# Layer 3 attention: one-bank units beside the scores, spread by a TensorE budget, with heads in another order

## The chip, the cores and the metric

One Trainium2 chip, of which the kernel uses one core. The metric is the device time of one execution in microseconds. The kernel before takes 4210.45 us, the median of three runs (4210.17 to 4224.06).

## The reference, cut to what matters

The program is a four-layer network on an input of 8 samples, 256 channels and 32 x 32 pixels, so 1024 tokens of 256 values in each sample. Everything is in fp32. The change lies in the attention of the last layer and in the routing of its mixture of experts:

```python
def _L3_attn_ref(x, qkv_w, qkv_b, proj_w, proj_b):   # x: (8, 1024, 256), normalised tokens
    ...                                              # 8 heads of 32
    scores = jnp.einsum('bnhd,bmhd->bhnm', q, k) * scale
    t = jnp.square(scores + C_SHIFT)                 # C_SHIFT = 5
    attn = t / jnp.sum(t, axis=-1, keepdims=True)
    out = jnp.einsum('bhnm,bmhd->bnhd', attn, v).reshape(B, N, D)
    return out @ proj_w.T + proj_b
...
t = t + _L3_attn_ref(_ln_t(t), ...)
t = t + _L3_ffn_ref(_ln_t(t), ...)                   # top 2 of 8 experts for each token
```

A weight of the attention is the square of a shifted score, so there is no exponential and no row maximum. The sum over keys of such squares is a quadratic form of q, and the kernel gets it from the 32 x 32 matrix of k times k, without summing the squares themselves.

## The kernel before, in words

`fast3` (from L2518) is the attention stage of layer 3. In the profiled execution it runs from about 2870 to 3842 us of the span. After it `fast3e` runs the experts to the end.

**A sample's attention.** `attention(b)` has 32 steps for a sample: two halves of the queries (`hh`, 512 each), two chunks of four heads (`c`), eight tiles of 128 keys (`kt`). Step i issues four score matmuls `s<-q,k` (L2684), one for each head on its own 32 rows of the array, into two PSUM pairs. A pair is two banks, 128 x 1024 fp32, for two heads. Two ACT squares `e<-s,five` of 128 x 1024 (L2690) empty them. Then `values(i - 1)` issues the four matmuls `A<-e,v` (L2668) of the step before, each on 32 columns of the array. I call the four matmuls of a step a quad. Eight steps add up in one bank A. After these, DVE writes `o<-A,r` (L2673), a product with the reciprocal r of the sum. After each second such group `proj` (L78 with `wo`) of four tiles goes into a pair, and DVE adds it to x (L2679).

**Work beside it.** While sample b runs, the generator `between(b)` prepares others, in this order:

- `routes.route(b - 1)` (from L2378) normalises the tokens of the sample just finished (`token_norm_steps`: statistics on DVE, `tn_r` on ACT, `mo_x` on DVE), adds them to x on POOL, sends both to DRAM, transposes them (`mo_xT`), computes the router's logits (`mo_l`), and then has a chain: a softmax (DVE, one exp on ACT, DVE), five DVE operations for the rank of each expert, choice and weights (to `both`), the counts `mo_n` on PE, and `cnt`, then sixteen small DVE operations that fill `place` and `carry`.
- `norm(b + 1)` loads x, normalises it to `xt` and transposes it to `xn`.
- `projections(b + 1)` makes q and k (`qk`, evacuated by ACT), v (by DVE), transposes of k (`kT`), G (products of k with itself), `Gq` (G times q, evacuated into `prod` by DVE) and `D` (the sum over a head, evacuated by ACT's Ln and turned round by Exp). Its two `D` evacuations also send r to DRAM.

In sample 0 `routes.fill()` follows, which issues eight large transfers `so<-zero` on SP.

**Order and PSUM.** Instructions stay on each engine in an order fixed when the program is built, except that the scheduler may move unpinned ones. `spread` (L1067) runs `attention(b)` and `between(b)` side by side, one count of yields against another: `between` has 19 yields for projections and 12 for route, over the 33 of a sample. After each sample everything left over is issued before the next begins. PSUM has three pairs (`own["S"]`, 6 banks), shared by the scores and everything beside them, and two one-bank buffers for A.

```python
def pair(name):
    return net.lent["pair"](name) if not own else own["S"].tile([P, 2, HF], F32, tag="S", name=name)

def bank(name):
    return pair(name)[:, 0]
```

`bank` is used before for G alone and takes a whole pair, using half.

Of the kernel before, what the change touches and what calls it, by code (L numbers as in the profile page):

```python
# [2306 lines left out]
class Routes:  # L2307
# [70 lines left out]
    def route(self, b, x, ones, pair):  # L2378
# [14 lines left out]
        for c in range(KC):  # L2393
            ps = pair("mo_xT").rearrange("p h n -> p (h n)")
            for t in range(NT):
                nc.tensor.transpose(ps[:, bass.ts(t, P)], xn[:, t, bass.ts(c, P)], net.ident)
            nc.vector.tensor_copy(xk[:, c, :], ps)
            yield

        pr = two.tile([P, NT, E8], F32, tag="pr", name="pr")  # L2400
        for t4 in range(0, NT, 4):
            ps = pair("mo_l")[:, 0]
            for i in range(4):
                net.linear(ps[:, bass.ts(i, E8)], xk, self.wr, bass.ts(t4 + i, P), slice(0, E8))
            nc.vector.tensor_copy(pr[:, t4 : t4 + 4], ps[:, : 4 * E8].rearrange("p (t e) -> p t e", e=E8))
            if not t4:
                yield
# [36 lines left out]
        ps = pair("mo_n")[:, 0]  # L2444
# [73 lines left out]
def fast3(net, io):  # L2518
# [4 lines left out]
    with ExitStack() as ctx, ExitStack() as tok, ExitStack() as att, ExitStack() as bef:  # L2523
# [41 lines left out]
        def norm(b):  # L2565
            x = xs[b] = xpool.tile([P, NT, C], F32, tag="x", name="x")

            (nc.sync if b else nc.scalar).dma_start(out=halves(x), in_=tokens(io.src[b]))
            yield
            xt = one.tile([P, NT, C], F32, tag="xt", name="xt")  # L2570
            yield from net.token_norm_steps(xt, x, norms, b > 0)
            yield
            xn = xns[b] = one.tile([P, KC, N], F32, tag="xn", name="xn")
            for c in range(KC):
                ps = pair("xn")
                for t in range(NT):
                    nc.tensor.transpose(ps[:, t // 4, bass.ts(t % 4, P)], xt[:, t, bass.ts(c, P)], net.ident)
                nc.vector.tensor_copy(xn[:, c, :], ps.rearrange("p h n -> p (h n)"))
                yield
            nc.gpsimd.tensor_tensor(x, x, bo.unsqueeze(1).to_broadcast([P, NT, C]), ALU.add)  # L2580

        def projections(b):
            xn = xns.pop(b)
            for d, w, bias, name in ((qs, wq, bq, "q"), (ks, wkk, bk, "k")):
                d[b] = own["two"].tile([P, KC, N], F32, tag=name, name=name)
                for c in range(KC):
                    ps = pair("qk")
                    for h in range(2):
                        net.linear(ps[:, h], w, xn, bass.ts(c, P), bass.ts(h, HF))
                    nc.scalar.activation(d[b][:, c, :], ps.rearrange("p h n -> p (h n)"), AF.Identity, bias=bias(c))  # L2590
                    yield
            v = vs[b] = own["two"].tile([P, NT, C], F32, tag="v", name="v")
            for t4 in range(0, NT, 4):
                ps = pair("v")
                for i in range(4):
                    net.linear(ps[:, i // 2, bass.ts(i % 2, C)], xn, wv, bass.ts(t4 + i, P), slice(0, C))
                nc.vector.tensor_copy(
                    v[:, t4 : t4 + 4].rearrange("p t c -> p (t c)"), ps.rearrange("p h n -> p (h n)")
                )
                yield  # L2600

# [3 lines left out]
            for t4 in range(0, NT, 4):  # L2605
                ps = pair("kT")
                for i in range(4):
                    for c in range(KC):
                        nc.tensor.transpose(
                            ps[:, i // 2, (i % 2) * C + c * P : (i % 2) * C + (c + 1) * P],  # L2610
                            ks[b][:, c, bass.ts(t4 + i, P)], net.ident,
                        )
                nc.vector.tensor_copy(
                    kt[:, t4 : t4 + 4, :, :P], ps.rearrange("p h (i c n) -> p (h i) c n", c=KC, n=P)
                )
                yield
            G = bank("G").rearrange("p (c n) -> p c n", c=KC)
            for c in range(KC):
                for t in range(NT):
                    nc.tensor.matmul(  # L2620
                        G[:, c, : P + 1], lhsT=kt[:, t, c, :P], rhs=kt[:, t, c, : P + 1],
                        start=(t == 0), stop=(t == NT - 1),
                    )
            gm = own["k2"].tile([P, KC, P + 4], F32, tag="gm", name="gm")
            nc.vector.tensor_tensor(gm[:, :, : P + 1], G[:, :, : P + 1], heads.to_broadcast([P, KC, P + 1]), ALU.mult)
            yield
            prod = one.tile([P, KC, N], F32, tag="xt", name="prod")
            r = rs[b] = own["two"].tile([P, KC, N], F32, tag="r", name="r")
            for c in range(KC):
                ps = pair("Gq")  # L2630
                for h in range(2):
                    nc.tensor.matmul(
                        ps[:, h], lhsT=gm[:, c, :P], rhs=qs[b][:, c, bass.ts(h, HF)], start=True, stop=True
                    )
                nc.vector.scalar_tensor_tensor(
                    prod[:, c, :], ps.rearrange("p h n -> p (h n)"), gm[:, c, P : P + 1], qs[b][:, c, :],
                    ALU.add, ALU.mult,
                )
                yield
            for c in range(KC):  # L2640
                ps = pair("D")
                for h in range(2):
                    nc.tensor.matmul(
                        ps[:, h], lhsT=heads[:, 0, :P], rhs=prod[:, c, bass.ts(h, HF)], start=True, stop=True
                    )
                nc.scalar.activation(
                    r[:, c, :], ps.rearrange("p h n -> p (h n)"), AF.Ln, scale=SCALE * SCALE, bias=rest
                )
                nc.scalar.activation(r[:, c, :], r[:, c, :], AF.Exp, scale=-1.0)
                nc.sync.dma_start(out=net.sums3[8 * b + 4 * c : 8 * b + 4 * c + 4, :], in_=r[0:P:32, c, :])  # L2650
                yield

        def attention(b):
            q, k, v, x = qs[b], ks[b], vs[b], xs[b]
            o = own["o"].tile([P, KC, N], F32, tag="o", name="o")
            steps = [(hh, c, kt) for hh in range(2) for c in range(KC) for kt in range(NT)]
            es, accs = {}, {}

            def values(i):
                hh, c, kt = steps[i]  # L2660
# [3 lines left out]
                if first:  # L2664
                    accs[0] = own["A"].tile([P, HF], F32, tag="A", name="A")
                A = accs[0]
                for h in range(NH):
                    nc.tensor.matmul(  # L2668
                        A[32 * h : 32 * h + 32], lhsT=v[:, kt, c * P + 32 * h : c * P + 32 * h + 32],
                        rhs=e[:, h, :], start=first, stop=last,  # L2670
                    )
                if last:
                    nc.vector.tensor_tensor(o[:, c, cols], A, rs[b][:, c, cols], ALU.mult)  # L2673
                    if c == KC - 1:
                        ps = pair("proj")
                        for t in range(4):
                            net.linear(ps[:, t // 2, bass.ts(t % 2, C)], o, wo, bass.ts(4 * hh + t, P), slice(0, C))
                        xh = x[:, 4 * hh : 4 * hh + 4].rearrange("p t c -> p (t c)")
                        nc.vector.tensor_tensor(xh, ps.rearrange("p h n -> p (h n)"), xh, ALU.add)  # L2679

            for i, (hh, c, kt) in enumerate(steps):
                ss = [pair("s") for _ in range(2)]
                for h in range(NH):
                    nc.tensor.matmul(  # L2684
                        ss[h // 2][:, h % 2], lhsT=k[32 * h : 32 * h + 32, c, bass.ts(kt, P)],
                        rhs=q[32 * h : 32 * h + 32, c, bass.ts(hh, HF)], start=True, stop=True,
# [6 lines left out]
                yield  # L2693
            values(len(steps) - 1)
            yield


        ROUTE = 12

        def between(b):  # L2700

            if b:
                yield from routes.route(b - 1, xs[b - 1], one, pair)
# [5 lines left out]
            else:  # L2709
                yield from net.head()  # L2710
# [8 lines left out]
        own["S"], own["A"] = io.pool(att, "f3s", 3, PSUM), io.pool(att, "f3v", 2, PSUM)  # L2719
        own["k1"], own["k2"] = io.pool(bef, "f3k", 1), io.pool(bef, "f3g", 2)  # L2720
        for _ in projections(0):
            pass
        for b in range(B):
            if b == B - 1:
                bef.close()
            beside = [(between(b), 19 * (b + 1 < B) + (ROUTE if b else 6))]
            for g, (first, last) in enumerate(GROUPS[:-1]):
                if b == last + 1:
                    beside.append((routes.sort(g), 1 + NT * (last - first)))
            spread((attention(b), 33), beside)  # L2730
        att.close()
        routing = routes.route(B - 1, xs[B - 1], one, lambda name: net.lent["pair"](name))
# [503 lines left out]
```

## Time and profile before

| what | value |
|---|---|
| time, median of 3 runs | 4210.45 us (4210.17 to 4224.06) |
| profiled execution, its own time | 4221.38 us |
| its span, mean granted clock of TensorE | 4219.6 us, 0.952 |
| PE, DVE, ACT, POOL busy over the span | 92%, 54%, 54%, 13% |
| layer 3 attention (first s to last step) | about 2870 to 3842 us |
| experts | 3842 to 4219.6 us |

Times inside the span are counted from its start. A matmul of fp32 leaves two records in the trace, so a quad of four heads is "x8". The profiler models the ends of matmuls and a few records are missing, so a busy PE is not always a PE at work; the start of one group to the start of the next is the safer measure. "idle before" names what the instruction waited for. A line such as `L78 PE MATMUL qk<-xn,w_l_wq` is the helper `linear`, and the names of the tiles tell which unit it is.

### The profile page before, as it was taken

How to read it: one execution, taken by the hardware profiler on the slowest of the kernel's cores; microseconds unless marked ns; L12 is line 12 of the kernel's file. 1: busy time of each engine (PE TensorE's matmuls, PEld its weight loads, DVE VectorE, ACT ScalarE, POOL GpSimd, SP SyncE). 2: the span in 40 equal slices, each digit the busy share in tenths (PEclk: the TensorE clock that was granted, in tenths of full speed). 3: DMA queues.
4: the chain of work that ended last, by engine and by line, in shares of the span. 5: the costliest groups of instructions: out<-in, count | busy, mean ns of one | idle time of the engine just before them, and what ended most of it. 6: DMA issues, size and time to landing. Idle time of an engine off the chain costs nothing. (4 is left out here: it accounts for less than half of the span.)

```text
span 4219.6 us, 52288 instructions
## 1 busy us (share of the span) xinstructions
PE 3866.5 (92%) x19430; PEld 1900.2 (45%) x19430; DVE 2297.3 (54%) x3994; ACT 2259.1 (54%) x3030; POOL 563.7 (13%) x645
## 2 busy tenths in 40 slices
PE   7999999999987788879999978989899999999997
PEld 3223333333333344444444435654344443436986
DVE  2368878878897488963222255842223333314455
ACT  3455655655554367743433445624655566666554
POOL 0000000000000000000000012440000050124763
PEclk9999999999998788889999989999999999999998
DMA  2222232232212468740100012430700040126676
GB/s 88 62 73 70 73 107 80 73 107 70 70 70 101 147 217 290 254 155 0 41 20 21 22 58 83 148 129 15 226 31 10 27 144 34 36 93 196 197 246 217
DMA packets 212346, 432.70 MB, mean 103 GB/s; under 512 B 26633, under 2 KB 137180, under 8 KB 199668
## 3 DMA queue, kind: packets, MB, share of 16 engines
q1 hardware_dynamic: 188980, 377.70, 27.1%
q0 software_dynamic: 19440, 46.45, 3.3%
q10 hardware_dynamic: 3664, 5.11, 0.4%
q8 instruction: 157, 2.57, 0.3%
q14 instruction: 105, 0.86, 0.1%
HBM read 257.56 MB, written 153.89 MB: 98 GB/s over the span
## 5 line engine op out<-in xcount | busy, mean ns | idle before, releaser
L2690 ACT ACTIVATE e<-s,five 128x1024 f32<-128x1024 f32 x512 | 538.8, 1110 | 277.9 <-PE s L2684 277.0
L1246 DVE SCALAR_TENSOR_TENSOR a<-hp,w_f_vec,a 128x961 f32<-128x961 f32 (+1 forms) x496 | 608.2, 1232 | 104.9 <-ACT a L1239 96.3
L2684 PE MATMUL s<-q,k 32*128 32x512 f32 x2048 | 348.6, 641 | 14.5 <-ACT e L2690 12.0
L1353 DVE TENSOR_TENSOR sum<-sum,e 128x1024 f32<-128x1024 f32 x192 | 230.4, 1218 | 149.2 <-ACT e L1399 149.2
L1399 ACT ACTIVATE e<-s 128x1024 f32<-128x1024 f32 x256 | 249.7, 1022 | 91.5 <-PE s L1393 82.1
L2668 PE MATMUL A<-e,v 128*32 128x512 f32 x2048 | 277.6, 606 | 0.3 <-ACT e L2690 0.3
L1357 PE MATMUL A<-e,va 128*32 128x512 f32 x2048 | 275.8, 620 | 0.0
L78 PE MATMUL pi<-xn,w_l_wpi 128*128 128x512 f32 x512 | 240.1, 610 | 13.7 <-ACT u L1500 9.2
L2684 PEld LDWEIGHTS s<-q,k 32*128 32x128 f32 x2048 | 111.4, 183 | 177.4 <-issue 94.2
L1393 PE MATMUL s<-q,k 32*128 32x512 f32 x1024 | 182.2, 648 | 2.4 <-ACT e L1399 2.4
L2837 PE MATMUL h<-xk,w 128*128 128x128 f32 x1192 | 152.7, 283 | 13.8 <-DVE xk L2823 13.8
L1704 PE MATMUL acc<-wt,z 128*64 128x192 f32 (+4 forms) x1344 | 128.5, 335 | 39.8 <-DVE wt L1759 39.3
L1026 POOL DMA_INDIRECT res<-y,to x149 | 148.6, 997 | 110.5 <-DVE y L2861 58.2
L78 PEld LDWEIGHTS pi<-xn,w_l_wpi 128*128 128x128 f32 x512 | 93.6, 193 | 149.5 <-issue 112.1
L2837 PEld LDWEIGHTS h<-xk,w 128*128 128x128 f32 x1192 | 150.6, 199 | 18.9 <-DVE xk L2823 14.1
L2806 ACT COPY w<-w_l3f_w 128x512 f32 x149 | 92.6, 625 | 115.8 <-PE h L2837 111.3
L1307 POOL MEMSET thrice<- 32x128 f32 x32 | 6.3, 196 | 1072.6 <-PE pe L1324 1072.6
L1438 ACT ACTIVATE hp<-pi,pib 128x512 f32<-128x512 f32 x128 | 87.1, 690 | 115.9 <-PE pi L78 115.9
L1324 PE MATMUL pe<-thrice,w_f_wpe 96*32 96x496 f32 (+1 forms) x768 | 130.7, 615 | 17.0 <-DMA thrice<-v 10.2
L2857 PE MATMUL y<-w_l3f_w,hid 128*128 x596 | 142.2, 381 | 0.3 <-ACT hid L2843 0.3
L1026 POOL DMA_INDIRECT so<-xl,rows x128 | 129.8, 1014 | 91.2 <-issue 50.4
L1357 PEld LDWEIGHTS A<-e,va 128*32 128x32 f32 x2048 | 61.9, 112 | 175.9 <-issue 175.3
(406 smaller groups left out, 6978.6 us busy)
## 6 DMA issues: line engine op xcount, KB each, us to landing
row<-shifts SPq DMA_DIRECT2D x144, 512.0 KB
x<-d SPq DMA_DIRECT2D x31, 1024.0 KB
xs<-so SPq DMA_DIRECT2D x73, 260.0 KB
so<-zero SPq DMA_DIRECT2D x5, 3380.0 KB
thrice<-v SPq DMA_DIRECT2D x256, 64.0 KB
gated<-st SPq DMA_DIRECT2D x32, 512.0 KB
hc<-gated SPq DMA_DIRECT2D x32, 512.0 KB
xl<-mox SPq DMA_DIRECT2D x64, 256.0 KB
```

What stands on the lines that cost most here:

```text
L78: self.nc.tensor.matmul(ps, lhsT=w[:, i, m], rhs=src[:, i, cols], start=(i == 0), stop=(i == k - 1))
L1026: made = self.nc.gpsimd.indirect_dma_start(**args)
L1246: nc.vector.scalar_tensor_tensor(to, fr, taps(t_), to, ALU.mult, ALU.add)
L1353: nc.vector.tensor_tensor(half, half, e[j], ALU.add)
L1357: nc.tensor.matmul(state["A"][32 * h : 32 * h + 32, c, :], lhsT=vas[b][:, kt, c, 32 * h : 32 * h + 32], rhs=e[h // 2][:, h % 2, :], start= ...
L1393: nc.tensor.matmul(ss[h // 2][:, h % 2], lhsT=ks[b][32 * h : 32 * h + 32, bass.ts(kt, P)], rhs=qs[b][32 * h : 32 * h + 32, bass.ts(gq, HF) ...
L1399: nc.scalar.activation(es[i][j], ss[j], AF.Exp, scale=SCALE)
L2668: nc.tensor.matmul(A[32 * h : 32 * h + 32], lhsT=v[:, kt, c * P + 32 * h : c * P + 32 * h + 32], rhs=e[:, h, :], start=first, stop=last,)
L2684: nc.tensor.matmul(ss[h // 2][:, h % 2], lhsT=k[32 * h : 32 * h + 32, c, bass.ts(kt, P)], rhs=q[32 * h : 32 * h + 32, c, bass.ts(hh, HF)], ...
L2690: nc.scalar.activation(e[:, 2 * j : 2 * j + 2], ss[j], AF.Square, scale=SCALE, bias=five)
L2837: nc.tensor.matmul(ps[:, j, m], lhsT=ws[j][:, k, bass.ts(m, P)], rhs=xk[:, j, k], start=(k == 0), stop=(k == KC - 1),)
L2857: nc.tensor.matmul(ps[:, j, :], lhsT=hid[:, j, k, :], rhs=w[:, k, :], start=(k == 0), stop=(k == KC - 1))
```

## The change

**What the diff does as text.** It inserts some 1800 lines inside `fast3`, with an older layer 3 attention and a second copy of many classes and functions. Python keeps the last definition of a name. So the first `fast3`, in which `bank` takes tiles of `own["X"]`, is replaced by a second one, and the other copies are the same as before apart from `Routes.route`. What runs is the last `Routes` and the last `fast3` (from L4322 of the new file; lines after the inserted text carry numbers some 1800 higher). In the last `fast3`, `pair` and `bank` are as shown above. A pool `own["X"]` of one bank is opened and no tile is taken from it.

**What runs differently.** Every unit beside the scores is a bank (512 columns) instead of a pair, each from `bank`. The loop of attention is one over all samples' 256 steps, with A in one buffer. At each step `others(i, used)` gives `between(b)` a budget of TensorE time, and each yield takes its cost from it. `between(b)` starts three steps after sample b's first. The heads of a step go in the order 2, 3, 0, 1, and all but the first are pinned. The core of the diff, against the code that ran before:

```diff
     def route(self, b, x, ones, bank):
         for c in range(KC):
-            ps = pair("mo_xT").rearrange("p h n -> p (h n)")
-            ...
-            yield
+            for h in range(2):
+                ps = bank("mo_xT")
+                for t in range(4):
+                    nc.tensor.transpose(ps[:, bass.ts(t, P)], xn[:, 4 * h + t, bass.ts(c, P)], net.ident)
+                nc.vector.tensor_copy(xk[:, c, bass.ts(h, HF)], ps)
+                yield 0.45
         ...
         for t4 in range(0, NT, 4):
-            ps = pair("mo_l")[:, 0]
+            ps = bank("mo_l")
             ...
-            if not t4:
-                yield
+            yield 1.7
```

In `norm` and `projections` the same is done to xn (yield 0.45), qk (1.7), kT (two tiles, 0.45), G (one chunk, 1.7), and the ends are interleaved:

```diff
+            for t2 in range(0, NT, 2):
+                values_of(t2)                        # v of two tiles, in one bank, copied by DVE
+                yield 1.7
+                product(t2 // 4, t2 // 2 % 2)        # Gq of 512 columns
+                yield 0.9
+            for c in range(KC):
+                for h in range(2):
+                    weights(c, h)                    # D of 512 columns, ACT's Ln; Exp and the DMA of r after h = 1
+                    yield 0.9
```

The attention:

```diff
-        def attention(b):
-            steps = [(hh, c, kt) for hh in range(2) for c in range(KC) for kt in range(NT)]
+        def attention(others):
+            steps = [(b, hh, c, kt) for b in range(B) for hh in range(2) for c in range(KC) for kt in range(NT)]
+            def together(h, ins):
+                if h != LATEST[0]:
+                    net.pinned(ins)
             ...
-                for h in range(NH):                  # in the quads of s and of A
+                for h in LATEST:                     # (2, 3, 0, 1), each through together()
             ...
-                    if c == KC - 1:                  # proj of four tiles, in a pair, at once
+                    if c == KC - 1:
+                        projects.extend((i + 2 + t2 // 2, b, hh, t2) for t2 in (0, 2))
             ...
                 if i:
                     values(i - 1)
-                yield
+                if projects and projects[0][0] <= i:
+                    project(*projects.pop(0)[1:])    # two tiles, in one bank
+                    others(i, 1.7)
+                else:
+                    others(i, 0.0)
```

The loop outside:

```diff
-        own["S"], own["A"] = io.pool(att, "f3s", 3, PSUM), io.pool(att, "f3v", 2, PSUM)
+        own["S"], own["A"] = io.pool(att, "f3s", 3, PSUM), io.pool(att, "f3v", 1, PSUM)
         ...
-        for b in range(B):
-            ...
-            spread((attention(b), 33), beside)
+        own["X"] = io.pool(att, "f3o", 1, PSUM)
+        PER = 4 * KC * KC * 2                        # 32 steps
+        IDLE, lines = 0.3, []
+        plan = {}
+        for b in range(B):
+            plan[PER * b + (3 if b else 0)] = [between(b), 0.0, 1.6 if b + 1 < B else 0.8]
+        ...
+        def others(i, used):
+            if i in plan:
+                lines.append(plan[i])
+            if lines:
+                line = lines[0]
+                line[1] += line[2] - used
+                while lines and line[1] > 0:
+                    cost = next(line[0], "over")
+                    ...                              # "over": the next line takes its place
+                    line[1] -= cost or IDLE
+            ...                                      # routes.sort in even parts, as before
+        attention(others)
```

A yield with no cost takes IDLE, 0.3, from a budget of 1.6 a step (0.8 in the last sample).

## The prediction

> **What bounds the kernel now.** First, in which engine's time the stage runs: busy time in windows of one sample each (columns: window, length, then busy time and instructions of PE, PEld, DVE, ACT, POOL, then clock, DMA share, GB/s).
> ```profile
> 3383.80:3508.70 124.90, 124.53 (x741) 51.80 (x740) 40.91 (x119) 76.60 (x77) 61.15 (x72) 1.00 0.42 124
> 3508.70:3633.30 124.60, 124.35 (x744) 51.88 (x743) 39.71 (x107) 76.59 (x77) 9.42 (x4) 1.00 0.07 26
> ```
> A sample takes 124.7 us, whether the sort on POOL and its transfers run (61 us of POOL, DMA 0.42) or not. PE is busy 99.7%, ACT 61%, DVE 33%: PE sets the time. But ends of matmuls are modelled, so hidden waits count as busy; only starts tell. Next, the PE timeline of steps beside other work, and of bare steps late in the last sample:
> ```profile
> 3119.86 1.14 PE L2684 MATMUL s<-q,k 32*128 32x512 f32 x8
> 3120.93 1.06 PE L2668 MATMUL A<-e,v 128*32 128x512 f32 x8
> 3121.93 1.98 PE L2643 MATMUL D<-prod,w_f_heads 128*128 128x512 f32 x4
> 3123.84 1.14 PE L2684 MATMUL s<-q,k 32*128 32x512 f32 x8
> ...
> 3817.47 1.38 PE L2684 MATMUL s<-q,k 32*128 32x512 f32 x8
> 3818.77 1.06 PE L2668 MATMUL A<-e,v 128*32 128x512 f32 x8
> 3819.77 1.23 PE L2684 MATMUL s<-q,k 32*128 32x512 f32 x8
> 3820.93 1.06 PE L2668 MATMUL A<-e,v 128*32 128x512 f32 x8
> 3821.92 1.38 PE L2684 MATMUL s<-q,k 32*128 32x512 f32 x8
> ```
> Start to start, a quad of s (four heads, two records each) takes 1.07, one of A 1.00, a D unit 1.91. Two bare steps take 4.45 us (3817.47 to 3821.92), 0.3 more than 2x2.07: ACT's two squares a step hold them.
> ```profile
> L2690 ACT ACTIVATE e<-s,five 128x1024 f32<-128x1024 f32 x512 | 538.8, 1110 | 277.9 <-PE s L2684 277.0
> ```
> 2x1.11 = 2.22, which is 4.45/2. So a sample is a PE sum. 32 steps 66.1; qk 4x3.63; v 2x3.65; proj 2x3.65; G 3.8; Gq and D 4x1.91; mo_l 2x1.95; 48 transposes 6.1; mo_n 0.6; two quads of s split by proj, 1.05 each: **119.3**. The other **5.4** are waits, nearly all on bare steps. In the whole stage (2870 to 3842) I sum 905 of 969.5; the 64 of waits are 32 in six middle samples, about 15 at the two ends, and one stall:
> ```profile
> 3034.36 1.13 PE L2684 MATMUL s<-q,k 32*128 32x512 f32 x4
> 3046.57 2.08 PE L2684 MATMUL s<-q,k 32*128 32x512 f32 x4 [11.08 <-ACT e L2690]
> ```
> 11 us, because e stands behind tn_r on ACT, which stands for x<-d, issued on SP after eight fills so<-zero; the clock then falls to half for about 12 us.
>
> **What the Trainium skill says.** "TensorEngine Tiling (Array Packing)", Key Properties: changing the tiling mode drains TensorE. The trace agrees: D's four matmuls cost 4x0.427 and 0.21 more, so each run of full-array work between s and A costs 0.21. "PSUM — Partial Sum Buffer", Engine vs sequencer instructions: ScalarE, VectorE and GpSimd queues are strict FIFO, and matmuls start in program order. The stall above agrees, and most of what follows rests on it. "TensorE: Matmul & The Clock Gate", HAM oscillation: idleness halves the clock; the trace shows it after 11 us of idling, and none after waits of 1 to 3 us, so I price none for those. "Perfetto Trace Analysis", Matmuls: independent groups should rotate through different PSUM banks, so that evacuation overlaps the next group. The change goes against it for A, and for more units on three pairs.
>
> **The change, part by part.** *What it says and isn't.* `own["X"]` is allocated, but `bank` still returns `pair(name)[:, 0]`, a tile of `own["S"]`. All units still take one of the three score pairs; they are half as big and twice as many. A falls from two buffers to one. So the scores get no pair more.
>
> *Work on PE.* Moved matmuls cost as before. By the order written out, runs of full-array work rise from 169 to 230: 61x0.21 = **+13**. Units fall inside quads of A: a lone head costs about 1.05, as a quad does, for some 20 part-quads **+21**. No proj unit splits s any more: **-10**. Sum **+24**, some 4 a middle sample (123.3).
>
> *ACT and DVE.* A 128x512 evacuation takes 0.69 (`hp<-pi` on ACT, o on DVE), against 1.11 and 1.22 for 1024. ACT gets 4x0.27 + 2x0.27 = 1.6 a sample on 76.6, DVE 12x0.16 = 1.9 on 40. Under PE's 124.7 they cost nothing by themselves. SP's transfers keep their order, fills ahead of x<-d, so the stall stays; POOL's two adds and its sort are the same.
>
> *The waits.* `spread` gave route one yield a step; the new budget charges a yield without PE work 0.3 of 1.6 us, so up to five of them fall in one step, and the PE work behind is issued too early. What route needs:
> ```profile
> 3155.28 0.19 DVE L2405 COPY pr<-mo_l 128x32 f32<-128x32 f32 x1 [3.76 <-PE mo_l L78]
> 3155.76 0.23 DVE L2410 TENSOR_TENSOR pr<-pr,red 128x64 f32<-128x64 f32 x1
> 3158.70 0.22 DVE L2414 TENSOR_REDUCE red<-pr 128x8 f32<-128x64 f32 x1 [2.72 <-ACT pr L2412]
> ...
> 3164.18 0.22 DVE L2441 TENSOR_TENSOR both<-chosen 128x64 f32<-128x64 f32 x1
> ...
> 3167.14 0.29 DVE L2449 COPY cnt<-mo_n 128x128 f32<-128x128 f32 x1 [1.76 <-PE mo_n L2447]
> ...
> 3166.44 0.43 PE L2446 MATMUL mo_n<-both,sooner 128*128 128x64 f32 x2
> ```
> Now mo_n comes 11.4 us after the last mo_l (five steps between) and waits for nothing. Each wait, a middle sample:
> - mo_n is issued two steps (4.4 us) after mo_l. The chain takes 1.0 to the subtraction, about 1.7 for exp between two squares on ACT, 5.2 to `both` (5.7 here, o's interruption taken off): 7.9. Wait 7.9-4.4 = **3.5**, with s and A of all later steps queued behind it.
> - The next A opens right behind. With one buffer it waits for o, and o stands on DVE behind cnt and sixteen place/carry operations of 0.20 (3.2 us): **2.4**. Each of the other three group ends costs A end to o end, 0.05 + 0.69; a quad of s and other units cover it.
> - xn's transposes come next. After o, DVE has four statistics and aggregates (2.2), tn_r and the first xt (0.9) to do, and one quad of A (1.0) is the cover: **2.1**.
> - mo_xT is issued one step (2.1) after the proj unit whose x it normalises. x takes 0.7, the last two tiles' statistics 0.7, tn_r on ACT between squares 2.2 (DVE idled 2.37 there), tn_r on DVE 0.2: 3.8, so **1.7**.
> - kT: three units on three pairs in a row, **0.9**; D: two in a row, their Ln between squares on ACT, **1.8**; Gq steps, 3.1 of PE against 3.5 for the pairs to turn round, over a few of them **1.0**.
>
> Sum 13.4 for 5.4 (the old bare steps vanish): +8.0, times six **+48**. In the first sample kT to G runs bare, 2 to 5, and the last has bare steps about as before: **+3**. Each term lies between 0 (what precedes it delays DVE's release too) and about half as much again.
>
> *Head order and pins.* A quad takes 1.07 whichever head leads, and waits of s for e other than the stall total 0.9: nothing; a loss up to 0.04 a step (10 in 256) is conceivable where the later pair now leads.
>
> Sum: 24 + 48 + 3 = **+75** on the profiled execution's 4221.4 (span 4219.6): 4296. That execution stands 10.9 above the median of the three runs shown, 4210.45, so **4285**.
>
> **The rivals.**
> - *Faster.* The even budget fills the bare steps and DVE's releases keep pace: no waits in middle samples (-32), and a part-quad costs its own matmuls only (+3 for +24): -29, **4181**. For: those 5.4 do lie on ACT-bound steps. Against: the chain to `both` is longer than its cover. It decides from below 1.4 us of waits a sample.
> - *About the same.* Waits partly hide in one another: 4 a sample for 5.4, -8, with +24: **4226**.
> - *Half the waits.* 9 a sample: 24 + 22 = **4256**.
> - *Scores alone on pairs.* Would save the kT, D and Gq waits, 22, and leave about 4260; the code's `bank` excludes it. The single A buffer stands either way.
>
> **How the numbers follow.** A measurement here tells about 0.5% from no change, 21 us: 4189 to 4231. My forecast 0.50; half the waits 0.26; about the same 0.17; faster 0.06; a little for what I don't see, slower too, 0.01. Slower by over 0.5% is thus 0.77. The range goes from 4222, a little under the third case, to 4322: waits half as large again (6x6.7 = 40) would end at 4325.
>
> **What would show it.** Right: the sample's period 136 rather than 124.7; PE waits named mo_n for both, A for o, xn for xt or tn_r; more part-quads of A; the stall near 3036 still there; ACT still at 1.11 an e. Wrong: period under 126; mo_n waiting for nothing; one-lone-head quads shorter than 0.6; s idle on e in every step (head order costing after all).

## The result, and the profile after

The changed kernel takes **4328.5 us** (median of 4 runs, 4322.4 to 4334.3). Before, measured again beside it, takes 4217.3 (4 runs, 4210.2 to 4228.0). The ratio is **1.0252** (95% interval 1.0222 to 1.0282): 111 us slower, where 75 were forecast. The time lies 6 us above the end of the range. The profiled execution has a span of 4320.7, which is 101.1 more than before's 4219.6.

The first s starts at 2870.2 before and at 2870.0 after, the last at 3839.2 and at 3933.7. So **94.7** of the 101.1 lie in the attention stage, and 6.6 behind it. First the windows of two samples after the change, in the columns of the prediction's windows (mo_n to mo_n):

```profile
3326.80:3468.90 142.10, 133.74 (x741) 52.73 (x741) 47.59 (x146) 78.47 (x83) 22.07 (x20) 0.94 0.10 31
...
3606.10:3743.00 136.90, 130.98 (x741) 52.17 (x741) 41.57 (x121) 78.57 (x83) 9.43 (x4) 0.96 0.04 16
```

A sample takes 137 to 143 us instead of 125. ACT grew from 76.6 to 78.5, as worked out, and bounds nothing. What is new is the clock, 0.94 and 0.96, where before has 1.00. The waits of PE in the stage (line, what it waited for: us in total, times, longest):

```profile
PE xn L4382 <- DVE xt L2823: 20.6, 4, 18.5
PE mo_n L4250 <- DVE red L4240: 19.3, 7, 3.4
PE A L4485 <- DVE o L4491: 10.5, 6, 3.1
PE mo_xT L4201 <- DVE mo_x L2823: 8.6, 6, 1.4
```

They are the waits that the prediction named, and mo_n's is 3.3 in the middle samples where 3.5 was forecast. But the PE timeline shows what follows them:

```profile
3326.84 0.41 PE L4250 MATMUL mo_n<-both,sooner 128*128 128x64 f32 x2 [3.30 <-DVE red L4240]
3327.08 0.39 PE L4251 MATMUL mo_n<-both,unit 128*128 128x64 f32 x2
3327.40 1.14 PE L4500 MATMUL s<-q,k 32*128 32x512 f32 x8
3328.47 1.78 PE L4485 MATMUL A<-e,v 128*32 128x512 f32 x8
3333.32 1.93 PE L4485 MATMUL A<-e,v 128*32 128x512 f32 x8 [3.07 <-DVE o L4491]
...
3338.08 1.54 PE L4382 MATMUL xn<-ident,xt 128*128 128x128 f32 x6
3339.55 2.29 PE L4500 MATMUL s<-q,k 32*128 32x512 f32 x6
```

PE waits 3.30 us at mo_n and 3.07 at A, and then a quad of A takes 1.93 instead of 1.06. Windows of 4 us give the granted clock (third number from the end):

```profile
3334.00:3338.00 4.00, 3.80 (x12) 0.79 (x4) 3.66 (x16) 0.51 (x2) 0.21 (x1) 0.50 0.00 0
3338.00:3342.00 4.00, 4.00 (x14) 2.09 (x14) 2.98 (x3) 0.34 (x1) 4.00 (x1) 0.50 0.00 0
```

The clock is at half, and PE counts as busy. I cut both stages into windows of 1 us and sum 1 minus the clock, less half of the idle time in them. That is what the halved clock costs. The work is counted in each trace and priced with the prediction's costs from start to start. The row of other waits is what remains. The stage adds up thus:

| stage, us | before (2870 to 3842) | after (2870 to 3936) | difference |
|---|---|---|---|
| matmul work at full clock | 903.5 | 927.4 | +23.9 |
| the stall on x of sample 2 | 11.1 | 18.5 | +7.4 |
| lost to the halved clock | 5.5 | 38.6 | **+33.1** |
| all other waits, hidden ones too | 51.9 | 81.5 | +29.6 |
| sum | 972 | 1066 | +94 |

Of the other waits the traces show 4 us before and 44 after as idle time of PE. The rest is hidden behind modelled ends, 47 and 37 us.

The halved stretches last 3.4, 6.8, 10.2, 17.1 or 27.3 us. That agrees with the window of about 3.4 us which the Trainium skill states ("TensorE: Matmul & The Clock Gate", What's actually happening). Its section HAM oscillation gives the rule of no idle gaps above that length. Here shorter gaps are followed by halved clock too: 3.3 us above, 2.9 and 2.2 in an experiment below (b2).

Two more lines of the PE timeline show the stall in sample 1 and the hand-over to the experts:

```profile
3049.44 0.69 PE L4382 MATMUL xn<-ident,xt 128*128 128x128 f32 x2 [18.50 <-DVE xt L2823]
...
3948.42 1.94 PE L4676 MATMUL a<-ident,xs 128*128 128x128 f32 x8 [6.53 <-DMA xs<-so]
```

Before, the first `a` starts 8.8 us after the last s, having waited 1.3. Now it starts 14.7 us after it, because the load xs<-so is issued at 3938.9, after the attention's end, behind twenty xl<-mox on SP. Before, it was issued at 3838.2, 1 us ahead of the last s.

### The profile page after: what moved, and what is told of

Same layout as the page of the kernel before. It is cut to its first block, busy times and chain, and to the rows that moved or that the text cites. A ratio compares the mean times of both kernels' runs of the same rounds, so it can differ in the third digit from the quotient of the medians.

```text
span 4320.7 us, 52471 instructions
## 1 busy us (share of the span) xinstructions
PE 3918.0 (91%) x19430; PEld 1903.4 (44%) x19430; DVE 2318.1 (54%) x4098; ACT 2274.3 (53%) x3078; POOL 563.9 (13%) x645
## 5 line engine op out<-in xcount | busy, mean ns | idle before, releaser
L4485 PE MATMUL A<-e,v 128*32 128x512 f32 x2048 | 310.0, 626 | 12.3 <-DVE o L4491 10.5
L4491 DVE TENSOR_TENSOR o<-A,r 128x512 f32<-128x512 f32 x32 | 22.1, 691 | 317.9 <-PE A L4485 317.9
L3128 PE MATMUL pe<-thrice,w_f_wpe 96*32 96x496 f32 (+1 forms) x768 | 128.5, 606 | 16.8 <-DMA thrice<-v 10.2
L4485 PEld LDWEIGHTS A<-e,v 128*32 128x32 f32 x2048 | 44.8, 109 | 219.3 <-issue 195.7
```

Of the source, the lines that this page charges most:

```text
L4485: nc.tensor.matmul(A[32 * h : 32 * h + 32], lhsT=vs[b][:, kt, c * P + 32 * h : c * P + 32 * h + 32], rhs=e[:, h, :], start=first, stop=last,),
```

## The experiments

Each group of runs had the kernel before beside it, on its chip. Its median was 4226.8 for the first four, then 4292.4, 4226.9 and 4287.1, so the ratios are what can be compared. The kernel before was traced once, so a few us between its stage and that of a later group mean little. The changed kernel stands at 1.0252 (1.0222 to 1.0282). The intervals of e1, e2, e4, e8 and e10 overlap with it, so for these the times alone decide nothing, and their traces are what is read. The kernels from e1 to e14 start from the changed kernel, e9 apart, without the text that Python replaces; their line numbers are those without it. b1, b2 and e9 start from the kernel before. "Halved clock" is the loss in us inside the stage.

**One buffer for A (e1).**

```diff
-        own["S"], own["A"] = io.pool(att, "f3s", 3, PSUM), io.pool(att, "f3v", 1, PSUM)
-        own["X"] = io.pool(att, "f3o", 1, PSUM)
+        own["S"], own["A"] = io.pool(att, "f3s", 3, PSUM), io.pool(att, "f3v", 2, PSUM)
```

> The changed kernel with two buffers for A again (and no pool X), nothing else. The changed kernel is 111 us slower than before (4328.5 to 4217.3). In its trace A waits for o 10.5 us in all, right after mo_n's waits, and the granted clock falls to half in stretches that cost about 39 us. Theory (waits plus a halved clock that follows idling): the 10.5 us go and the stretches get shorter, some 20 us less, 4305 to 4312; mo_n still waits 3.3 us a sample. Rival (the halved clock comes from thin work, the 8-column logits and the transposes, not from idling): 10 us less, 4318, and the stretches as long as they were.

Measured: 1.0219 (1.0187 to 1.0252). The ratio is the one that the theory gave, but not for its reason, and the interval takes in the rival's too. No wait for o is left, but xn's waits grow from 20.6 to 28.9, and the halved clock still costs 34.9. What A waited for, xn now waits for: the same DVE queue.

**The distance to mo_n (e2).**

```diff
     (the five yields between the last mo_l and mo_n, in route)
-        yield
+        yield 1.6
-            plan[...] = [between(b), 0.0, 1.6 if b + 1 < B else 0.8]
+            plan[...] = [between(b), 0.0, 1.8 if b + 1 < B else 0.8]
```

> The changed kernel, but each of the five yields of the router's chain is charged 1.6 of the budget, which is 1.8 instead of 1.6 a step: mo_n is issued five steps after the last mo_l, as before, instead of two. A keeps one buffer. Theory (mo_n's wait, and the halved clock that follows idling): mo_n waits for nothing, most stretches of halved clock go, 19 us of waits and 20 to 30 of clock less, 4280 to 4290. Rival (thin work halves the clock): 19 us less, about 4310, the stretches still there after the transposes. Rival (the wait only moves on to A and xn behind DVE's sixteen place operations): under 10 us less.

Measured: 1.0230 (1.0199 to 1.0261). This is the second rival. The waits of PE:

```profile
PE A L2681 <- DVE o L2687: 20.4, 6, 3.6
PE xn L2578 <- DVE xt L1019: 16.2, 6, 6.0
```

mo_n waits for nothing, and A waits twice as long for o. The halved clock costs 38.2 as before the edit. One link of the chain was cut free, and the next took its place.

**Both (e3).**

> Both edits: two buffers for A, and mo_n five steps after mo_l. Theory: no wait for mo_n or o, the clock full outside the first sample's stall, about 55 us less than the changed kernel: 4265 to 4275, still 50 above before from units, part-quads, the longer stall and the hand-over to the experts. Rival (units and part-quads cost more than thought, waits less): 4290 to 4300.

Measured: 1.0170 (1.0131 to 1.0209), 66 us above before. The theory's 48 to 58 us above before lie at the low end of the interval (55 to 88), and the rival's 73 to 83 inside it, so the rival isn't excluded. Halved clock 16: in three middle samples one stretch of 6.8 us each, after xn has waited 1.9 to 2.6, and none in two others, where it waited 2.1. The wait of PE for xt (11.7 is the stall in sample 1):

```profile
PE xn L2578 <- DVE xt L1019: 22.5, 6, 11.7
```

**TensorE kept busy while mo_n waits (e4).**

```diff
+        if b + 1 < B:
+            for _ in range(4):
+                net.pinned(nc.tensor.matmul(net.filler[0], lhsT=net.ident, rhs=net.filler[1], start=True, stop=True))
         ps = bank("mo_n")
         ...                                   (and net.filler: the idle bank of X, and the weights wq)
```

> The changed kernel with four matmuls of 128x512 that nothing reads in front of each mo_n of the first seven samples (into the idle bank X, 3.4 us of PE): mo_n is issued as late as it was, but TensorE isn't idle while it waits. Theory (idling halves the clock): the stretches of halved clock after mo_n go although the waits' length stays, 15 to 30 us less than the changed kernel, 4300 to 4313. Rival (thin work before it halves the clock): stretches stay, the time within 5 us of 4328. Rival (the fillers delay mo_n): 5 to 10 us slower.

Measured: 1.0246 (1.0205 to 1.0286), halved clock 36.6. Nothing was decided: the idle time only went on to A, which waits up to 3.8 us for o. Most stretches begin in that wait or just behind it. Two of 3.4 us (3172.8 and 3179.6) begin with no wait near them.

**The same with two buffers for A, and fillers at xn too (e10).**

```diff
+        def filled(name, n):
+            ps = pair(name)
+            for _ in range(n):
+                net.pinned(nc.tensor.matmul(ps[:, 1], lhsT=net.ident, rhs=wq.rearrange("p k o -> p (k o)"), start=True, stop=True))
+            return ps[:, 0]
-        ps = bank("mo_n")
+        ps = net.filled("mo_n", 4) if b + 1 < B else bank("mo_n")
-                    ps = bank("xn")
+                    ps = filled("xn", 4) if b > 2 and not h and not c else bank("xn")
```

> The changed kernel with two buffers for A and four matmuls of 128x512 that nothing reads (3.4 us) ahead of mo_n and, from sample 3 on, ahead of the first transposes xn; they write the unused half of the pair that the unit has anyway. So TensorE idles neither at mo_n nor at xn. Theory (idling halves the clock): outside the first sample's stall the clock stays full, 20 to 30 us of halved clock gone, but up to 10 us of fillers that are not hidden: about 4300. Rival (thin work, logits and transposes, halves the clock): stretches stay, 4318 or slower.

Measured: 1.0218 (1.0189 to 1.0247), the ratio of e1 and between the two expectations. The halved clock falls from 34.9 to 23. From 3097 to 3376 and from 3384 to 3785 there is none at all, with the logits and the transposes unchanged. So thin work alone didn't halve it there. But it can: in the same trace stretches of 3.4 us begin at 3055.4 and 3912.2 with no idle time in the 3.4 us before them, as one does at 3018.1 in the changed kernel. All three follow the 8-column matmuls mo_l. So neither theory holds alone; the last section puts the two together. The fillers, twelve times 3.4 us of PE, cost what they saved, as they are longer than some of the waits.

**The wait in the kernel before (b2).** This is the cleanest of them: half-size units, one A, budget and pins are all absent.

```diff
         net.pinned(nc.scalar.activation(pr, pr, AF.Exp))
-        yield
         ...                                   (the next two yields of the chain go too)
```

> The kernel before, with three of the five yields between the router's logits and mo_n left out, so that mo_n is issued two to three steps after the last mo_l instead of five. Units, A's two buffers and the scheduling are those of before. Theory (a wait of 3 us is followed by a stretch of halved clock): mo_n waits about 3 us in seven samples, and stretches of 3 to 10 us of halved clock follow each; 7x(3+3) less 15 of bare-step waits, 20 to 35 us slower than before. Rival (the halved clock comes with the change's half-size units): waits, but a full clock, 5 to 15 us slower.

Measured: 1.0108 (1.0081 to 1.0135), 44 us slower than before, more than the theory's 20 to 35. The rival's full clock isn't seen. The PE timeline:

```profile
3332.77 0.66 PE L2443 MATMUL mo_n<-both,sooner 128*128 128x64 f32 x2 [2.86 <-DVE red L2433]
...
3333.79 5.42 PE L2681 MATMUL s<-q,k 32*128 32x512 f32 x16
3339.14 1.94 PE L2665 MATMUL A<-e,v 128*32 128x512 f32 x8
3341.01 1.63 PE L2681 MATMUL s<-q,k 32*128 32x512 f32 x8
3342.57 1.06 PE L2665 MATMUL A<-e,v 128*32 128x512 f32 x8
```

A single wait, 2.87 us in six samples and 2.23 in the seventh, and with each a stretch of 6.8 or 10.2 us at half clock, which begins late in the wait or within 2 us of its end. In the stage that is 20 us of waits and 35 lost to the clock, where before loses 5.5. The middle samples go from 125 to 135 us. Here a wait of 3 us costs two to three times its length, without any part of the change.

**What the change's words say (e5).**

```diff
         def bank(name):
+            if "X" in own:
+                return own["X"].tile([P, HF], F32, tag="X", name=name)
             return pair(name)[:, 0]
```

> The changed kernel with a bank() that takes its tiles from the pool X once it is open, so that the score pairs serve the scores alone; A keeps one buffer. This is what the change's words say. Theory (the waits are those of DVE's chain and of A; the clock follows): mo_n, mo_xT and o wait as before; units now queue on one bank, whose evacuation takes 0.7 us, while hidden waits on pairs (about 4 us a sample) go: within 15 us of the changed kernel, 4315 to 4340. Rival (pairs shared with units are what costs): 25 to 35 us faster, below 4305.

Measured: 1.0540 (1.0504 to 1.0576). Both theories miss. The halved clock costs 118 us of the stage, more than half of it from mo_xT to mo_n, where no idle time is shown ahead of mo_n's own wait. The PE timeline there:

```profile
3234.24 1.12 PE L2397 MATMUL mo_xT<-ident,mo_x 128*128 128x128 f32 x4
3235.28 2.07 PE L2698 MATMUL s<-q,k 32*128 32x512 f32 x2
3237.29 1.12 PE L2397 MATMUL mo_xT<-ident,mo_x 128*128 128x128 f32 x4
```

Units of four transposes stand between single heads of s: a quad is cut up, and a head alone takes 2.0 us from start to start at half clock. A sample takes 158 to 170 us. So lending pairs to the units was not the cost, and one bank for all of them is a large one.

**The stall (b1).**

```diff
+        def load(b): ...                      (the tile and the DMA of x, taken out of norm)
                 if b == 0:
+                    load(2)
                     yield from routes.fill()
```

> The kernel before, with the load of x for sample 2 issued ahead of the eight fills on SP. Theory (x<-d queued behind the fills makes the 11 us stall in sample 1, and the stall halves the clock): stall and stretch go, 12 to 17 us faster than before. Rival (x comes early but the norm then waits for something else): 0 to 5 us.

Measured: **0.9974** (0.9961 to 0.9987), 11 to 14 us faster than before. No wait over 2.6 us is left in the stage, and the interval around the stall, 141.9 from mo_n to mo_n in the first pair of samples, becomes 126.3. The longest waits left are these, for e:

```profile
PE s L2688 <- ACT e L2694: 3.9, 3, 2.6
```

It beats both kernels. Halved clock isn't gone from the stage: three other stretches of 3.4 or 6.8 us are left, which cost 8.

**One A in the kernel before (e9).**

```diff
-        own["S"], own["A"] = io.pool(att, "f3s", 3, PSUM), io.pool(att, "f3v", 2, PSUM)
+        own["S"], own["A"] = io.pool(att, "f3s", 3, PSUM), io.pool(att, "f3v", 1, PSUM)
```

> The kernel before with one buffer for A instead of two, nothing else. Theory (one buffer costs only where o stands behind other work on DVE; at an ordinary group end the next A waits 0.75 us for o, of which a quad of s hides all): 0 to 8 us slower than before, no wait of A for o above 1 us. Rival (one buffer is itself a main cost of the change, at 32 group ends): 20 to 40 us slower, with halved clock after the waits.

Measured: 1.0064 (1.0045 to 1.0083), 27 us slower, which is the rival's size, and the waits are above the theory's 1 us too. But the reason is the theory's: only one group end a sample waits, where o falls behind the five rank operations on DVE. PE's and then DVE's timeline:

```profile
3290.99 1.13 PE L2668 MATMUL A<-e,v 128*32 128x512 f32 x8 [2.95 <-DVE o L2673]
...
3289.43 0.69 DVE L2427 TENSOR_REDUCE rank<-gt 128x64 f32<-128x512 f32 x1
3290.15 0.20 DVE L2432 TENSOR_SCALAR chosen<-rank 128x64 f32<-128x64 f32 x1
3290.26 0.68 DVE L2673 TENSOR_TENSOR o<-A,r 128x512 f32<-128x512 f32 x1
```

Six such waits are 17.5 us. The other group ends show none. The clock is halved behind four of the six, for 3.4 or 6.8 us, and behind two not at all; in the stage the halved clock costs 15, where before loses 5.5. So a wait of 3 us isn't always followed by as much as in b2.

**Pins and head order (e7, e8).**

```diff
 e7:             def together(h, ins):
-                if h != LATEST[0]:
-                    net.pinned(ins)
+                net.pinned(ins)
 e8:             (none pinned, and)
-        LATEST = (2, 3, 0, 1)
+        LATEST = (0, 1, 2, 3)
```

> The changed kernel with all four heads of a quad pinned instead of three, so that no unit falls inside a quad of A: the built order has 2 part-quads in place of 43. Theory (a part-quad costs like a quad, but the work of all parts is a small term, and the chain to mo_n is untouched): 5 to 20 us faster than the changed kernel's 1.0252 of before, 1.0205 to 1.024. Rival (the parts fill what would be waits, and go over into waits): within 3 us, 1.0245 to 1.026.

> The changed kernel with the heads of a quad in the order 0, 1, 2, 3 and none pinned, as before the change. Theory (order and pins of heads are worth nothing): within 6 us of the changed kernel, 1.0235 to 1.0265 of before. Rival (the order gains, as the pair whose bank comes last is asked for first): 10 to 25 us slower, over 1.0275. Rival (the pins cost part-quads): 10 us faster, under 1.023.

Measured: e7 1.0193 (1.0168 to 1.0218), e8 1.0255 (1.0229 to 1.0280). The order with its three pins is worth nothing that the intervals tell, as priced. In e8's trace the waits are others, though (A waits 12 us for e and mo_n 8 instead of 19), so gains and losses may cancel. Pinning all four heads gains some 25 us, by the intervals about 8 to 41, so not clearly more than the 5 to 20 expected. Its trace shows what the pins do: runs of full-array work fall from 233 to 208, no quad of A is cut up but for one, and the stage without its idle time and halved clock is 24 us shorter. But xn waits 44.5 us in all, 24 more, and the halved clock costs 40. So in this execution, one of the slower ones, the stage is only 8 us shorter.

**Four edits together (e12)** (two buffers, mo_n's distance, all pins, x loaded first).

> The changed kernel with four edits: A in two buffers, mo_n five steps after mo_l, all heads pinned, and x of sample 2 loaded ahead of the fills. What is left of the change is one-bank units, the budget and the late proj. Theory (waits, the clock that follows them, part-quads and the stall are the cost; the rest is near nothing): 25 to 45 us above before, 1.006 to 1.011, with xn still waiting 2 us a sample and the clock halved after it. Rival (half-size units themselves cost): 60 us or more, over 1.014. Below 0.997 it would beat both kernels.

Measured: 1.0126 (1.0098 to 1.0154), between the two expectations. xn waits 3.6 to 4.3 us in each middle sample and mo_xT 1.4, and the clock is halved after each: 38 us in the stage.

**The price of a yield (e14, e13).** Two numbers change, once in the changed kernel alone and once on top of two buffers, all pins and x loaded first.

```diff
-        IDLE, lines = 0.3, []
+        IDLE, lines = 1.6, []
-            plan[...] = [between(b), 0.0, 1.6 if b + 1 < B else 0.8]
+            plan[...] = [between(b), 0.0, 2.1 if b + 1 < B else 1.6]
```

> The changed kernel with two numbers changed: a yield without TensorE work is charged 1.6 instead of 0.3, and the budget is 2.1 a step instead of 1.6 (1.6 in the last sample). In the built order xn now comes four steps after mo_n, mo_xT three steps after proj, mo_n four to five after mo_l. A keeps one buffer, the heads' order and pins stay. Theory (the budget's price of 0.3 makes all chains too short, and the clock follows the waits): no wait for mo_n, xn or mo_xT in middle samples, the period 126 to 129 us, 1.006 to 1.012 of before, the rest being one-buffer waits as in before with one A and the stall. Rival (half-size units cost): over 1.018.

> The same pacing with A in two buffers, all heads pinned and x of sample 2 loaded ahead of the fills. One-bank units, their order and the late proj stay. Theory: no waits of TensorE but those on ACT, no stall, no halved clock in the middle samples, the period 122 to 125 us: 0.993 to 1.002 of before. Rival (half-size units cost): 1.008 or more.

Measured: e14 **1.0018** (1.0007 to 1.0030), e13 0.9987 (0.9973 to 1.0000). Two numbers take back nearly all of the 111 us, with one A, one-bank units, pins and head order as the change has them. e14 does better than its theory, and e13's ratio is as expected. Which of the two numbers does it, the price or the budget, was not told apart. The windows of two samples of e14 and the waits of its PE:

```profile
3207.70:3332.40 124.70, 122.39 (x744) 50.35 (x740) 41.53 (x120) 78.35 (x84) 9.40 (x4) 1.00 0.07 26
3332.40:3462.30 129.90, 125.92 (x745) 51.48 (x741) 46.52 (x156) 78.30 (x84) 23.34 (x24) 0.99 0.12 38
```

```profile
PE A L2681 <- DVE o L2687: 7.4, 5, 1.7
PE s L2696 <- DVE cnt L2449: 5.8, 1, 5.8
PE xn L2578 <- DVE xt L1019: 4.4, 4, 2.3
```

mo_n and mo_xT wait for nothing on DVE in the stage any more. The gain isn't waits and clock alone. Against the changed kernel e14's stage is 79 us shorter: 36 of idle time, 23 of halved clock, and 20 of the rest, as units now stand side by side more often (179 runs of full-array work for 233, 266 parts of A for 272). In e13 two samples take 122.5 and 122.2 us, where before's middle ones take 124.3 to 125.1. Bare steps are not much fewer (74 in the stage for 90), but no quad of s is split by proj any more, where before has 15 lone heads; at 1.05 each that is 16 us, an estimate, and the likelier source, not shown. Other samples of e13 take up to 137, with a wait of 6.1 for cnt. In the trace cnt stands on DVE behind the statistics of the next x, ahead of which DVE idles for 5.6 us until 3440.5; that x was issued on SP at 3431.8, so its load is the likely cause. The halved clock still costs 15 in e14 and 14 in e13. e13 doesn't differ from b1 beyond the intervals.

## Why the prediction was wrong in its size

**What held.** The direction and the mechanism: `bank` still takes pairs, DVE's chains are longer than the two steps that the budget leaves, and everything behind mo_n, A, xn and mo_xT stands with them. e14 shows the budget, with its price of 0.3, to be the cause. Single terms held too. Work was +24 and is +23.9, counted in the trace at the prediction's own prices. mo_n's wait was 3.5 and is 3.3. mo_xT's was 1.7 and is 1.44. The stall stayed. Head order and its pins together were nothing that e8 can tell.

**What failed, first: a price of zero.** "None after waits of 1 to 3 us, so I price none for those": the clock. It costs 33 us more than before, and this is the step that failed. Its reading of the trace is wrong. The stage has no wait between 1 us and 11 before, so it showed nothing either way. The rest of the same trace shows the contrary: of 75 waits of 1 to 3 us that begin at full clock, 39 have the clock halved within them or in the 4 us behind. One stands in the experts (PE's timeline, then a window):

```profile
4128.56 2.89 PE L2837 MATMUL h<-xk,w 128*128 128x128 f32 x16 [2.91 <-DVE xk L2823]
4129.60:4133.00 3.40, 3.40 (x17) 3.22 (x16) 3.33 (x8) 2.06 (x6) 2.15 (x3) 0.50 0.67 210
```

So an upper bound was due: a wait of 3 us and with it up to 10 us at half clock, 5 us in each of six samples.

**Second: waits added up as if each stood alone.** The sum of 13.4 a sample was 80 us in six samples, and 32 of old waits were to vanish, which made +48. Measured, waits other than the stall and the clock are +30: 40 more that the trace shows, and only 10 fewer hidden ones. The 5.4 a sample weren't nearly all on bare steps: before's middle samples have 8 or 9 of these, each about 0.17 over its 2.07. o's wait is 0.9 to 3.1, not always 2.4. xn's 2.1 is 0.2 behind A's wait in the sample shown. For kT and D the trace shows 1.7 us in all. One queue, DVE's, serves mo_xT, mo_n, o and xn, so the first wait pays for the next ones. e1, e2 and e4 show it: whatever was taken away came back one link further on. The rival "half the waits" came nearest on this point, and the period of 137 in the later samples agrees with the forecast 136 only because the two errors cancel.

**Third: the ends.** The stall was taken as unchanged, with 3 us for all the ends. It grew by 7.4, and the hand-over to the experts, which I didn't price, costs about 6. Together, the clock is 33 us above the forecast, the ends 11 above it and the waits 18 below it, which makes the 26 between +75 and the +101 of the profiled executions. That it isn't more is luck: the errors cancel in part. Another 7 us of the distance from 4285 to 4328.5 are the level, as the kernel before took 4210.45 in the three runs known then and 4217.3 beside the change.

**Half-size units** cost nothing of their own that these runs can tell. In e14 and e13 they are all there.

## What to carry to other kernels

When a scheduler spreads work by one engine's time, the steps that use none of that engine still need a price, namely the latency of their chain, or the next step that does use it will stand. A short wait on TensorE is to be priced at its length plus half the stretch at half clock that may follow: for one of 3 us that was 3 to 5 us in b2, and none to 3 in e9. Look for such waits in the whole trace, not only in the stage that changes. Waits on one in-order queue aren't summed: cutting one moves it to the next link, so undo all of a chain, or its cause, before judging.

## What wasn't expected of the hardware

A wait of 2.2 to 2.9 us, alone, was followed by 6.8 or 10.2 us at half clock in seven samples out of seven (b2), and one of 2.7 to 3.0 by 3.4 or 6.8 us in only four of six (e9). In each trace all changes of the clock lie on one grid of 3.41 us, and a wait can fall into one window of it or across two. Cut along the grid, the attention stages of the sixteen traces have 4539 windows at full clock. The next window is at half clock behind 71 of the 73 in which PE idles for more than 55%, 37 of the 73 with 40 to 55%, and 49 of the 4393 with less.

Of these last, 31 show next to no idle time, and 28 of them hold the logits mo_l, matmuls of 8 columns; the other three hold transposes beside s. An estimate of the work in a window sorts both kinds: 0.427 us for a record of 512 columns (the prediction's price from D), less in proportion to the columns, and a quarter for one head of a quad. Where this comes to 40% of the window or more, none of 4237 is followed by half clock; below 15%, 37 of 38 are; between, 120 of 264. So idling and thin work look like one cause, too little work in a window. This was found in the traces afterwards, and no run was made to test it.

In e5 the clock stayed at half for 27 us in a stretch with no idle time shown, while units alternated with parts of quads on one bank. The skill's section A second HAM failure mode describes small idle times between groups that make the clock go back and forth. This trace shows the clock, not such idle times, since ends are modelled. The estimate gives these windows 5 to 35% of work, but for the last, with 46%, behind which the clock is full again.
